# Two-layer group-norm network on one core: both norms two steps later in their bands, the first layer's maps of an image's first band two steps later

## The chip, the cores and the metric

The kernel runs on one core of one Trainium2 chip, in one launch. The metric is the device time of that launch in microseconds (us). Five engines work side by side, each through its own queue in order: PE (TensorE, matrix products), DVE (VectorE), ACT (ScalarE), POOL (GpSimd) and SP (SyncE), which here only issues DMA transfers. [...]

## The reference

The input `x` has 8 images of 256 channels of 64x64 pixels in 32-bit floats. Two layers follow one another, each with a residual:

```python
x = x + _L0_conv_ref(_gn(x), ...)
x = x + _L1_conv_ref(_gn(x), ...)
```

`_gn` is a group norm over 32 groups of 8 channels: every image needs its mean and variance before its first pixel can be normalised.

Layer 0 computes, for every pixel, its own 3x3 filter for each of 32 groups. Two 1x1 maps of 32 channels, `x1` and the 3x3 unfolded `x2`, go through a norm with constants, a relu, a 1x1 convolution to 32 channels ("hidden"), again norm and relu, and a last 1x1 convolution gives 9 weights for each group. The third map `x3` has 256 channels, and the output is the sum of its nine neighbours, each times its weight:

```python
out = jnp.einsum('bgskhw,bgkhw->bgshw', x3u, w)
```

Layer 1 has two branches that are added with rates. One is an attention of 4 heads of 64 channels in which each pixel looks at its 7x7 neighbours (reflected at the rim), with a position term on the keys. The other is a softmax over 9 weights for each channel and pixel, from one 1x1 convolution, that weighs depthwise convolutions (3x3, relu, 3x3) of the layer's input.

## The kernel before, in words

**Tiling.** An image is cut into `NB` = 8 bands of 8 rows, 512 pixels each; 256 channels are two halves of 128 partitions. The main loop runs over `g` = 8 x image + band. While layer 1 works on band `g`, layer 0 is `AHEAD` = 12 bands ahead: in band 0 of an image it makes the maps of band 4 of the next one. The 12 bands before the first (`g` below 0, "alone") have layer 0 only. Both halves and four pieces make 8 steps in a band (`s` = 0 to 7).

**The order is written out by hand.** Nothing is moved by a scheduler: every engine receives its instructions in the order in which the program calls for them. Each step has six places, each ended by `advance()`. `after(n, f)` calls `f` at the n-th place from now. `steer(g, s)` runs at the beginning of a step and starts the norms and the loads of the input. `beside(g, s)` returns two lists of side work for the step: `mid`, called at the third place, whose matmuls are issued there and whose follow-up on ACT or DVE comes a place later; and `end`, called at the last. One entry is an exception: `small_maps` is called where it is appended to `mid`, ahead of the step's score matmuls, and only its follow-up `write_maps` comes with the rest.

**A step in the second layer.** PE multiplies queries with keys (L703) and, for an earlier step, probabilities with values (L747). DVE takes the maximum (L712), ACT the exponential (L720), DVE the reciprocal of the sum (L727), ACT scales the probabilities (L729), and a step later PE transposes them (L735), which ACT copies out (L737). Twice in a step PE makes branch weights `pf` (8 matmul records of 512 columns in all in the trace, L825), and ACT takes their exponential `ex` (L830), which POOL adds up (L1026, L838) and DVE divides (L850). The depthwise convolutions (L773 to L818) are spread over DVE with their first tap and relu on ACT. Side work of layer 1 is the values (L563, with copies of their windows to `vc` on ACT: L572, L577, L581; transposed at L607 and copied at L609), the queries (L637, L641) and the keys (L658; DVE L666 and L673; reflection L683).

**Layer 0 in a band.** `small_maps` multiplies the band with the scaled weights `w12s` (L328), ACT writes the result as eight pieces (L343 or L347), POOL copies their edges (L351 to L358). `value_maps` does the same for each half of `x3` with `w3s` (L369, ACT L374) and stores it to DRAM (L375). `hidden_maps` is called for the band before, with its hidden activations on ACT (L418), the convolution on PE (L429) and what follows at set places later. `values_by_group` loads `x3` back in another layout (L389 to L397, six transfers). `tap_weights` works two bands behind the maps: weights on PE (L447), products on DVE (L460), sums on POOL (L468).

**The norms.** Both use `gn_affine`: DVE joins the statistics (L231), PE averages over groups (L237), DVE works out the variance (L246 to L250), PE again, DVE (L258), ACT takes a square root (L262), DVE the reciprocal and offset (L266, L269). Each stage waits a number of places, the square root standing about 14 places behind the start. `scaled_weights` folds layer 0's norm into its weights: at the end of the chain DVE scales `w12` and `w3` (L296, L297, twice each), PE makes the bias terms (L304), DVE writes them (L312, L314). It is started in band 3, for the image after next. `norm_rows` makes the norm of layer 1 for the next image in band 6; its last steps bring it to every channel (L512 to L524), and the first rows that need it are normalised in bands 7 and 0.

**Buffers.** Nearly all matmul results go through five PSUM buffers with the tag `gen`, used in turn in program order: the next user waits until the reader of the user five places before is done. The scores and the accumulators have PSUM of their own.

The starts of the pieces that the change touches stand in these lines:

```python
if s == (2 if g >= 0 else 3) and i == NB - 2 and 0 <= b + 1 < B:
    norm_rows(b + 1)
n = g + AHEAD + 1
if s == 2 and n % NB == 0 and 0 < n < B * NB:
    scaled_weights(n // NB)
...
if s == 0 and g + AHEAD < B * NB:
    mid.append(small_maps(*divmod(g + AHEAD, NB)))
```

Of the kernel before, what the change touches and what calls it, by code (L numbers as in the profile page):

```python
# [25 lines left out]
NB = H // R  # L26
# [34 lines left out]
AHEAD = NB + 4  # L61
# [25 lines left out]
def conv_layers_kernel(ctx: ExitStack, tc: tile.TileContext, ins: dict, out: bass.AP):  # L87
    nc = tc.nc
    x_in = ins["x"]
    B = x_in.shape[0]  # L90
# [124 lines left out]
    def after(n, f):  # L215
        later.append((place[0] + n, f))
# [399 lines left out]
    def position(b, i):  # L616

        first, last = new_keys(i)
        n, a = last - first, i * R + first
        pe = images[b].pe[i] = w1.tile([P, KW - PAD, W], F32, tag="pe", name=f"pe_{b}_{i}", bufs=1)  # L620
        nc.gpsimd.tensor_add(
            pe[:, :n],
            pecol.unsqueeze(1).to_broadcast([P, n, W]),
            perow[:, a : a + n].unsqueeze(2).to_broadcast([P, n, W]),
        )
# [240 lines left out]
        after(5, quotient)  # L866


    def beside(g, s):

        b, i = divmod(g, NB)
        bn, inx = divmod(g + 1, NB)
        mid, end = [], []

        early = i in (0, NB - 1)
        if g >= 0:
            if s == 2 - early:
                mid.append(lambda: queries(b, i, 1))
            if s == 3 - early:
                mid.append(lambda: keys(b, i, 1))  # L880
        early = inx in (0, NB - 1)
        if 0 <= g + 1 < B * NB:
            if s == 5 - early:
                mid.append(lambda: position(bn, inx))
            if s == 6 - early:
                mid.append(lambda: queries(bn, inx, 0))
            if s == 7 - early:
                mid.append(lambda: keys(bn, inx, 0))

        if g >= 0 and i < NB - 1:  # L890
            if s in (4, 5):
                mid.append(lambda: values(b, i + 2, s - 4))
            if s in (6, 7):
                end.append(lambda: value_tile(b, i + 2, s - 6))
        if g > 0 and i and s in (0, 1):
            mid.append(lambda: value_tile(b, i + 1, s + 2))
        if i == NB - 1 and 0 <= b + 1 < B:
            if s in (4, 5):
                mid.append(lambda: values(b + 1, 0, s - 4))
            if s in (6, 7):  # L900
                end.append(lambda: value_tile(b + 1, 0, 2 * s - 12))
                end.append(lambda: value_tile(b + 1, 0, 2 * s - 11))
        if g >= 0 and i == 0:
            if s == 0:
                mid += [lambda: values(b, 1, 0), lambda: values(b, 1, 1)]
                end.append(lambda: value_tile(b, 1, 0))
            if s in (1, 2):
                mid.append(lambda: value_tile(b, 1, 2 * s - 1))
            if s == 1:
                end.append(lambda: value_tile(b, 1, 2))  # L910

        nxt = [(b, i + 2, 0)] if g >= 0 and i + 2 < NB else []
        if i == NB - 1 and 0 <= b + 1 < B:
            nxt = [(b + 1, 0, 0), (b + 1, 1, 1)]
        for bb, ii, d in nxt:
            if s == d:
                end.append(lambda bb=bb, ii=ii: load_rows(bb, ii))
            if s in (d + 1, d + 2):
                end.append(lambda bb=bb, ii=ii, d=d: normalise(bb, ii, s - d - 1))

        alone = g < 0
        if 0 <= g + AHEAD < B * NB:
            bq_, iq = divmod(g + AHEAD, NB)
            if alone and s == 0:
                mid.append(lambda: small_maps(bq_, iq)())
            if s == (2 if alone else 0):
                (mid if alone else end).append(lambda: value_maps(bq_, iq, 0))
            if s == (3 if alone else 1):
                mid.append(lambda: value_maps(bq_, iq, 1))
        if 0 <= g + AHEAD - 1 < B * NB and s == (2 if alone else 1):  # L930
            at = (3, 7, 8, 12, 16) if alone else (5, 13, 14, 19, 21)
            end.append(lambda: hidden_maps(*divmod(g + AHEAD - 1, NB), at))
        if 0 <= g + AHEAD - 2 < B * NB and s in TAPS_AT[alone]:
            u = TAPS_AT[alone].index(s)
            end.append(
                lambda: tap_weights(*divmod(g + AHEAD - 2, NB), u, g < -1, PRODUCTS_AT[g < -1][u])
            )
        return mid, end

    def steer(g, s):  # L940

        b, i = divmod(g, NB)
        if s == (2 if g >= 0 else 3) and i == NB - 2 and 0 <= b + 1 < B:
            norm_rows(b + 1)
        n = g + AHEAD + 1
        if s == 2 and n % NB == 0 and 0 < n < B * NB:
            scaled_weights(n // NB)
        if s == (3 if g < -1 else 7) and g + AHEAD0 < B * NB:
            first_stats(*divmod(g + AHEAD0, NB), n=40 if g < -1 else 9)
        if s == 5 and 0 <= g + 1 < B * NB:  # L950
            bn, inx = divmod(g + 1, NB)
            xr = images[bn].xr[inx] = x_tile("xr", bn, inx)
            nc.sync.dma_start(out=xr, in_=images[bn].x1[inx].rearrange("(t p) n -> p t n", p=P))
        if s == (0 if g < 0 else 4) and 0 <= g + 1 + AHEAD < B * NB:
            bn, inx = divmod(g + 1 + AHEAD, NB)
            if inx not in images[bn].xc:
                images[bn].xc[inx] = load_x(bn, inx, "xc")
        if s == 5 and 0 <= g - 1 + AHEAD < B * NB:
            values_by_group(*divmod(g - 1 + AHEAD, NB))
        if s == 4 and 0 <= g - 1 + AHEAD < B * NB:  # L960
            x_by_group(*divmod(g - 1 + AHEAD, NB), g < -2)

    with tc.manual_schedule():
# [21 lines left out]
        for g in range(-AHEAD, B * NB):  # L985
            b, i = divmod(g, NB)
            for s in range(STEPS):
                ct, m = divmod(s, NT // 2)
                mid, end = beside(g, s)
                steer(g, s)  # L990
                if g >= 0:
                    if s == 0 and g + AHEAD < B * NB:
                        mid.append(small_maps(*divmod(g + AHEAD, NB)))
                    nm = f"{b}_{i}_{ct}_{m}"
                    sco = score_tile(nm)
                    weighted = [(a, weighted_values(*a, pt, sco)) for a, pt in pending]
                    prob, nmax = scores(b, i, ct, m, sco)
                    for a, po in weighted:
                        add_values(*a, po)
                    pending = [] if before is None else [(before[:-1], transposed(nm, before[-1]))]  # L1000
                    tot = exponentials(nm, prob, nmax)
                advance()
                if g >= 0:
                    ex, exb = w1.tile([P, 2, BAND], F32, tag="ex", name=f"ex_{nm}", bufs=3), ex if m else None
                    branch_weights(b, i, ct, m, 0, ex)
                    if m in (0, 2):
                        todo = list(conv[0])
                    for _ in range(2):
                        todo.pop(0)()
                advance()  # L1010
                if g >= 0:
                    probabilities(prob, tot)
                rest = [f() for f in mid]
                advance()
                for f in rest:
                    if f:
                        f()
                if g >= 0:
                    for _ in range(2 if m % 2 == 0 else len(todo)):
                        todo.pop(0)()  # L1020
                    before = (b, i, ct, m, prob)
                advance()
                if g >= 0:
                    branch_weights(b, i, ct, m, 1, ex)
                    if exb is not None:
                        after(4, lambda ex=ex, exb=exb: nc.gpsimd.tensor_add(ex, ex, exb))  # L1026
                    if m == 1:
                        conv[1]()
                        conv = depthwise_middle(b, i, ct)
                    if m == NT // 2 - 1:  # L1030
                        oc = depthwise_end(b, i, ct, conv[1])
                        after(4, lambda a=(b, i, ct, ex, oc): dynamic_sum(*a))
                if s % 4 == 3 and 0 <= (g * NCT + ct + 1) < B * NB * NCT:
                    gn, cn = divmod(g * NCT + ct + 1, NCT)
                    conv = depthwise_begin(*divmod(gn, NB), cn)
                advance()
                for f in end:
                    f()
                advance()
# [90 lines left out]
```

## Time and profile before

| | |
|---|---|
| median of 3 runs | 4153.6 us (4153.14 to 4155.73) |
| the profiled execution | 4152.64 us |
| its span in the profile | 4150.9 us |
| mean granted clock of PE in it | 0.993 |
| busy PE / DVE / ACT / POOL | 97% / 87% / 74% / 70% |
| a band of image 2, from first score matmul to the next band's | 59.3 to 68.8 us |

The profile is of one execution. Its span runs from the first instruction to the last; the execution's own time has 1.74 us around it. "Busy" is the time in which an engine had an instruction in work, as a share of the span, register and DMA-issuing instructions left out. A line such as L825 is a line of the kernel's file. A group of instructions is named by line, engine, operation and by what it writes and reads; the number of instructions stands behind an x. In the list of waits an engine's idle time is summed by the instruction that ended it: which instruction was late, how often, and the longest of these waits. A line of the timeline gives the start and the duration, the engine and the instruction, and in square brackets the wait ahead of it with what ended it.

### The profile page before, as it was taken

To read this page: it belongs to the slowest core of one execution; us is meant where nothing else is said; L and a number is where in the kernel's file an instruction comes from. 1 tells how busy PE (TensorE), PEld (TensorE's weight loads), DVE (VectorE), ACT (ScalarE), POOL (GpSimd) and SP (SyncE) were. 2 spreads that over 40 slices of the span, in tenths; PEclk is the share of its full clock that TensorE was granted. 3 is DMA by queue.
4 is the path that set the end of the run, shared out by engine and by line. 5 is a ranking of instruction groups with operands and counts; after the bars stand their busy time and mean duration, and the time that the engine had idled before them with its cause. 6 is when DMAs were issued, how large, how long until landed. Compare 5 with 4: busy or idle time off the path is not lost.

```text
span 4150.9 us, 72735 instructions
## 1 busy us (share of the span) xinstructions
PE 4022.6 (97%) x25292; PEld 2126.8 (51%) x25292; DVE 3591.9 (87%) x7248; ACT 3081.0 (74%) x7726; POOL 2923.0 (70%) x1902
## 2 busy tenths in 40 slices
PE   6789999999999999999999999999999999999998
PEld 3345555555555555555555555555555555455554
DVE  5878998899898898889998898888988889977777
ACT  3467778777787777877778777777778777687776
POOL 4767777677786777777777777777777677744554
PEclk8999999999999999999999999999999999999999
DMA  8854234234244233334234234244233233111100
GB/s 226 194 135 111 73 91 109 72 94 109 62 101 107 76 94 98 81 94 109 72 85 118 72 94 105 66 101 106 71 82 99 65 87 85 33 41 39 39 28 21
DMA packets 381264, 367.89 MB, mean 89 GB/s; under 512 B 55648, under 2 KB 282720, under 8 KB 380640
## 3 DMA queue, kind: packets, MB, share of 16 engines
q1 hardware_dynamic: 377568, 358.68, 34.3%
q8 instruction: 200, 3.28, 0.3%
q10 hardware_dynamic: 3328, 4.55, 0.3%
q14 instruction: 168, 1.38, 0.1%
HBM read 261.42 MB, written 101.71 MB: 87 GB/s over the span
## 4 chain that ended last, share of the span: by engine, by line
PE 71%; DVE 14%; POOL 6%; ACT 5%; DMA 2%; issue 2%; SPq 1%; POOLq 0%; ACTq 0%; DVEq 0%
PE pf L825 33%; PE ptp L735 5%; PE sco L747 5%; PE pk L658 5%; PE sco L703 5%; PE p L369 5%; DVE prod L460 4%; PE pq L637 4%; POOL xg L468 3%; PE pvt L607 2%; PE pv L563 2%; DVE acc L808 2%; PE pw L447 2%; DVE acc L782 2%; POOL ex L1026 2%
## 5 line engine op out<-in xcount | busy, mean ns | idle before, releaser
L825 PE MATMUL pf<-yp,c_wfc 128*128 128x512 f32 x4096 | 1930.5, 595 | 10.6 <-ACT vc L581 5.0
L468 POOL TENSOR_TENSOR xg<-xg,prod 128x1024 f32<-128x1024 f32 x549 | 1203.9, 2193 | 96.6 <-DVE prod L460 64.1
L825 PEld LDWEIGHTS pf<-yp,c_wfc 128*128 128x128 f32 x4096 | 729.9, 190 | 690.5 <-issue 619.4
L1026 POOL TENSOR_TENSOR ex<-ex,ex 128x1024 f32<-128x1024 f32 x384 | 907.7, 2364 | 61.9 <-ACT ex L830 57.2
L830 ACT ACTIVATE ex<-pf 128x512 f32<-128x512 f32 x1024 | 607.3, 593 | 297.9 <-POOL ex L1026 141.3
L782 DVE SCALAR_TENSOR_TENSOR acc<-yp,c_chan,acc 128x504 f32<-128x504 f32 (+3 forms) x1104 | 766.2, 694 | 42.3 <-ACT acc L773 21.7
L460 DVE SCALAR_TENSOR_TENSOR prod<-pw,c_par,x3q 128x1040 f32<-128x1040 f32 x576 | 733.9, 1281 | 66.8 <-PE pw L447 21.6
L808 DVE SCALAR_TENSOR_TENSOR acc<-hid,c_chan,acc 128x504 f32<-128x504 f32 (+3 forms) x1024 | 757.8, 740 | 20.2 <-ACT acc L802 2.1
L855 POOL TENSOR_TENSOR ex<-ex,rec 128x512 f32<-128x512 f32 x127 | 162.3, 1278 | 809.5 <-DVE rec L850 767.1
L729 ACT ACTIVATE prob<-prob,tot 128x196 f32<-128x196 f32 x1024 | 411.6, 450 | 387.2 <-DVE tot L727 386.4
L712 DVE CUSTOM_DVE_ANT_0 prob<-sco,c_mask 128x196 f32<-128x196 f32 x1024 | 325.5, 355 | 272.4 <-PE sco L703 272.0
L720 ACT ACTIVATE prob<-prob,nmax 128x196 f32<-128x196 f32 x1024 | 461.4, 454 | 46.9 <-DVE nmax L712 45.3
L747 PEld LDWEIGHTS sco<-pt,vt 112*64 112x64 f32 x8160 | 283.8, 137 | 182.3 <-issue 51.7
L737 ACT COPY pt<-ptp 112x512 f32<-112x512 f32 x511 | 297.0, 581 | 105.0 <-PE ptp L735 103.0
L735 PE MATMUL ptp<-ident,prob 128*112 128x128 f32 x2044 | 341.7, 287 | 31.2 <-ACT prob L729 30.5
L747 PE MATMUL sco<-pt,vt 112*64 112x64 f32 x8160 | 347.0, 227 | 0.0
L735 PEld LDWEIGHTS ptp<-ident,prob 128*112 128x112 f32 x2044 | 203.9, 133 | 201.4 <-issue 77.7
L703 PE MATMUL sco<-kb,qb 64*64 64x196 f32 x4096 | 295.2, 357 | 0.0
L563 PE MATMUL pv<-yp,c_wv 128*128 128x512 f32 (+2 forms) x576 | 247.3, 554 | 0.6
L369 PE MATMUL p<-xc,w3s 128*128 128x512 f32 x512 | 244.4, 601 | 0.0
L658 PE MATMUL pk<-yp,c_wk 128*128 128x512 f32 (+2 forms) x576 | 240.8, 545 | 0.0
L637 PE MATMUL pq<-yp,c_wq 128*128 128x512 f32 x512 | 240.6, 592 | 0.0
(140 smaller groups left out, 5294.0 us busy)
## 6 DMA issues: line engine op xcount, KB each, us to landing
x<-x3n SPq DMA_DIRECT2D x128, 264.0 KB, 2.1
x3q<-x SPq DMA_DIRECT2D x128, 264.0 KB, 7.2
xc<-in_x SPq DMA_DIRECT2D x64, 512.0 KB, 5.0
xg<-in_x SPq DMA_DIRECT2D x256, 128.0 KB, 4.8
x<-xg SPq DMA_DIRECT2D x256, 128.0 KB, 2.4
yp<-x SPq DMA_DIRECT2D x128, 256.0 KB, 3.3
xr<-x SPq DMA_DIRECT2D x64, 512.0 KB, 5.8
out_x<-xr SPq DMA_DIRECT2D x64, 512.0 KB, 3.1
```

What stands on the lines that cost most here:

```text
L369: nc.tensor.matmul(p3, im.w3s[:, kt, mt * P : (mt + 1) * P], im.xc[i][:, kt, :], start=(kt == 0), stop=(kt == NCT - 1),)
L460: nc.vector.scalar_tensor_tensor(prod[:, :, :RUN], pw[:, j, :RUN].unsqueeze(1).to_broadcast([P, SHARE, RUN]), par[:, PCB2 + k : PCB2 + k + 1],
L468: nc.gpsimd.tensor_add(im.xg[i], im.xg[i], rows(prod))
L703: nc.tensor.matmul(sco[half[t], h, :NKEY], qb[half[h], 2 * m + t].rearrange("p r c -> p (r c)"), kb[half[h], :, c0 : c0 + KW], start=True, ...
L720: nc.scalar.activation(prob[:, h, :NKEY], prob[:, h, :NKEY], AF.Exp, bias=nmax[:, h : h + 1], scale=-1.0, accum_out=tot[:, h : h + 1],)
L735: nc.tensor.transpose(ptp[:, h, ch], prob[:, h, ch * CHUNK : (ch + 1) * CHUNK], ident)
L747: nc.tensor.matmul(po[half[h], :, t * TQ : (t + 1) * TQ], im.vt[i + ch, m][:n, t, (2 * ct + h) * HD : (2 * ct + h + 1) * HD], pt[:n, h, ch ...
L782: nc.vector.scalar_tensor_tensor(o, yp[:, ct, ra + dr : rb + dr, ca + dc : cb + dc], chan[:, ct, CW1 + k : CW1 + k + 1], o, ALU.mult, ALU.add,
L808: nc.vector.scalar_tensor_tensor(o, hid[:, ra + dr : rb + dr, ca + dc : cb + dc], chan[:, ct, CW2 + k : CW2 + k + 1], o, ALU.mult, ALU.add,)
L825: nc.tensor.matmul(pf, wfc[:, kt, 2 * m + j, ct * P : (ct + 1) * P], images[b].yp[i][:, kt, PAD : PAD + R], start=(kt == 0), stop=(kt == N ...
L830: nc.scalar.activation(ex[:, j].rearrange("p (r c) -> p r c", r=R), pf, AF.Exp)
L1026: after(4, lambda ex=ex, exb=exb: nc.gpsimd.tensor_add(ex, ex, exb))
```

## The change

Three pieces of work are issued at other steps; no instruction is added, removed or altered.

- `norm_rows` is started at step 4 of band 6 for step 2 (seven bands: images 0 to 6).
- `scaled_weights` is started at step 4 of band 3 for step 2 (six bands: images 0 to 5). In the bands ahead of the first image both stay where they were.
- In band 0 of an image (seven bands, images 0 to 6) `small_maps` goes from step 0 to step 2, the two halves of `value_maps` from the end of step 0 and the middle of step 1 to the middles of steps 3 and 4, `hidden_maps` from the end of step 1 to that of step 3, and `values_by_group` from step 5 to step 6. The other bands keep theirs: `maps_at` returns 0 for them.

```diff
@@ -865,6 +865,10 @@
 
         after(5, quotient)
 
+
+    def maps_at(g):
+
+        return 0 if g % NB else 2
 
     def beside(g, s):
 
@@ -923,11 +927,15 @@
             bq_, iq = divmod(g + AHEAD, NB)
             if alone and s == 0:
                 mid.append(lambda: small_maps(bq_, iq)())
-            if s == (2 if alone else 0):
-                (mid if alone else end).append(lambda: value_maps(bq_, iq, 0))
-            if s == (3 if alone else 1):
+            if alone:
+                at = 2, 3
+            else:
+                at = maps_at(g) + (1 if i == 0 else 0), maps_at(g) + (2 if i == 0 else 1)
+            if s == at[0]:
+                (mid if alone or i == 0 else end).append(lambda: value_maps(bq_, iq, 0))
+            if s == at[1]:
                 mid.append(lambda: value_maps(bq_, iq, 1))
-        if 0 <= g + AHEAD - 1 < B * NB and s == (2 if alone else 1):
+        if 0 <= g + AHEAD - 1 < B * NB and s == (2 if alone else maps_at(g) + 1):
             at = (3, 7, 8, 12, 16) if alone else (5, 13, 14, 19, 21)
             end.append(lambda: hidden_maps(*divmod(g + AHEAD - 1, NB), at))
         if 0 <= g + AHEAD - 2 < B * NB and s in TAPS_AT[alone]:
@@ -940,10 +948,10 @@
     def steer(g, s):
 
         b, i = divmod(g, NB)
-        if s == (2 if g >= 0 else 3) and i == NB - 2 and 0 <= b + 1 < B:
+        if s == (4 if g >= 0 else 3) and i == NB - 2 and 0 <= b + 1 < B:
             norm_rows(b + 1)
         n = g + AHEAD + 1
-        if s == 2 and n % NB == 0 and 0 < n < B * NB:
+        if s == (4 if g >= 0 else 2) and n % NB == 0 and 0 < n < B * NB:
             scaled_weights(n // NB)
         if s == (3 if g < -1 else 7) and g + AHEAD0 < B * NB:
             first_stats(*divmod(g + AHEAD0, NB), n=40 if g < -1 else 9)
@@ -955,7 +963,7 @@
             bn, inx = divmod(g + 1 + AHEAD, NB)
             if inx not in images[bn].xc:
                 images[bn].xc[inx] = load_x(bn, inx, "xc")
-        if s == 5 and 0 <= g - 1 + AHEAD < B * NB:
+        if s == (6 if g >= 0 and i == 0 else 5) and 0 <= g - 1 + AHEAD < B * NB:
             values_by_group(*divmod(g - 1 + AHEAD, NB))
         if s == 4 and 0 <= g - 1 + AHEAD < B * NB:
             x_by_group(*divmod(g - 1 + AHEAD, NB), g < -2)
@@ -989,7 +997,7 @@
                 mid, end = beside(g, s)
                 steer(g, s)
                 if g >= 0:
-                    if s == 0 and g + AHEAD < B * NB:
+                    if s == maps_at(g) and g + AHEAD < B * NB:
                         mid.append(small_maps(*divmod(g + AHEAD, NB)))
                     nm = f"{b}_{i}_{ct}_{m}"
                     sco = score_tile(nm)
```

## The prediction

> **What bounds the kernel now.** I read the page's busy shares first, then the list of waits, then image 2's bands in the timeline. A step is counted from its first score matmul (L703).
>
> ```profile
> PE 4022.6 (97%) x25292; PEld 2126.8 (51%) x25292; DVE 3591.9 (87%) x7248; ACT 3081.0 (74%) x7726; POOL 2923.0 (70%) x1902
> ACT prob L729 <- DVE tot L727: 386.4, 266, 6.4
> POOL x L351 <- ACT x L343: 166.0, 55, 28.2
> ```
>
> PE is the bound; only what lets it idle, or adds to it, moves the end. ACT and DVE wait long in the list, but PE feels that only where the wait reaches it. Windows over band 0 (first line), 1, 3 and 6 of image 2:
>
> ```profile
> 1246.27:1315.04 68.77, 66.73 (x410) 34.84 (x406) 58.05 (x121) 51.42 (x133) 44.85 (x29) 1.00 0.34 84
> 1315.04:1376.60 61.56, 61.07 (x392) 31.99 (x388) 55.31 (x107) 46.61 (x116) 46.72 (x32) 1.00 0.38 93
> 1438.20:1502.10 63.90, 62.73 (x412) 33.60 (x410) 59.70 (x125) 49.20 (x118) 46.85 (x32) 1.00 0.36 90
> 1625.70:1685.00 59.30, 59.20 (x397) 32.90 (x395) 54.84 (x117) 47.95 (x132) 45.88 (x30) 1.00 0.34 82
> ```
>
> After the time come PE, PEld, DVE, ACT and POOL busy. PE is idle 2.04 us in band 0, 0.49 in band 1, 1.17 in band 3, 0.10 in band 6. The bands are in step to a few hundredths across images, so a band's gain or loss counts about seven times (six for the weights' norm). A restart hides a little more: four 512-column records issue in 1.72 us, and against that pace band 0 loses about 3.3 us: 0.6 in step 0, 0.25 in step 5, 1.65 in step 6, 0.8 in step 7. Its worst place and its step 0 in the timeline:
>
> ```profile
> 1298.65 0.81 ACT L729 ACTIVATE prob<-prob,tot 128x196 f32<-128x196 f32 x2 [4.84 <-DVE tot L727]
> 1299.17 0.78 PE L735 MATMUL ptp<-ident,prob 128*112 128x128 f32 x4 [1.44 <-ACT prob L729]
> ...
> 1254.52 0.34 ACT L581 COPY vc<-pv 128x16 f32<-128x16 f32 x3
> 1254.91 0.54 PE L607 MATMUL pvt<-ident,vc 128*112 128x128 f32 x3 [0.15 <-ACT vc L581]
> ```
>
> PE waits for ACT's probabilities (L729), which wait for DVE's reciprocal (L727): DVE is late. In step 0 PE waits for ACT's window copies (L581).
>
> [...] in the scaling of the weights in band 3 (DVE, then POOL beside it):
>
> ```profile
> 1476.16 0.24 DVE L296 TENSOR_SCALAR w12s<-c_w,sc_a 128x64 f32<-128x64 f32 x1
> 1476.32 1.41 DVE L297 TENSOR_SCALAR w3s<-c_w,sc_a 128x256 f32<-128x256 f32 x1
> 1477.65 2.17 DVE L296 TENSOR_SCALAR w12s<-c_w,sc_a 128x64 f32<-128x64 f32 x1
> 1479.74 1.18 DVE L297 TENSOR_SCALAR w3s<-c_w,sc_a 128x256 f32<-128x256 f32 x1
> ...
> 1476.31 1.27 POOL L838 TENSOR_TENSOR ex<-ex 128x512 f32<-128x512 f32 x1
> 1477.54 2.23 POOL L468 TENSOR_TENSOR xg<-xg,prod 128x1024 f32<-128x1024 f32 x1
> 1479.73 1.04 POOL L621 TENSOR_TENSOR pe<-pecol,perow 128x512 f32<-128x512 f32 x1
> ```
>
> Each DVE instruction ends just after a POOL one: 4.76 us for the four. Before POOL is at work, at 25 us, the same four take 0.93. [...] the trace has 1.28 us before Sqrt (L262) and again before the next Exp (L830), so a norm costs ACT 2.77 us wherever it stands.
>
> **The change, part by part.** Nothing is added or removed; instructions change places on all queues. Durations are those of the profiled execution, 4150.9 us of span and 1.74 around it (4152.64); the median of 4153.6 lies 0.96 higher, and the sum is added to the median.
>
> 1. **Maps in band 0** (seven bands). PE loses L328 (0.92 us) ahead of step 0, L369 (1.72) at the end of step 0 and 1.72 in step 1; L328 comes back before step 2, L369 in steps 3 and 4. The hidden maps' matmuls (0.58 and 0.36) go from the ends of steps 3 and 4 to those of 5 and 6. ACT's eight map activations (L343/L347, 463 ns median, 3.82 us in a row) go from step 0 to step 2, x3n (688 ns) and the hidden activations (0.80) two steps later. I walk the queues, keeping durations:
>  - Step 0: the L607 transposes wait for ACT's copies, which end at 1254.75 with no map ahead of them. They stay where they are, so the 0.92 is lost. The two L369 are a gain: step 2 begins 2.56 us earlier, 1.72+1.72-0.92 and rounding.
>  - Step 2: the maps now hold a PSUM buffer of "gen", so the second pf waits for DVE's L673 on the keys: 0.41 us. On ACT the maps stand behind the vt copy of a transpose that PE finishes at 1270.8, and before pf's Exp, L683, L543, L737 and step 3's L720: 71.5+3.8+0.6+0.5+1.1+0.6+1.0, about 1279.1. L720 ended at 1278.7 before. DVE's L727 waits for it in order, with 2.5 us idle, and runs when it ran before (1279.12), while PE is 1.1 us early in step 4. L818 and L773 then come 0.6 later, and so do DVE's taps (1282.6 for 1281.97).
>  - Steps 4 to 6: PE's extra 1.72+0.58-0.36 is eaten by that. L735 of step 6 comes at about 1299.65 (1299.17 before). The next pf now takes the buffer that ACT's vc copies free 2.15 us after L729 begins, so 1301.25, where it began at 1299.78. In return step 7's 0.8 is gone. The band ends near 1316.05 for 1315.04: **+1.0, times 7 = +7**. Bounds: 0 if the buffer wait does not bite, +2 if DVE falls further back.
>  - POOL: the edge copies (L351 to L358) wait in step 2 instead of step 0; POOL waits 3.3 us for a product at 1284.9 anyway, so they cost nothing; without that cover they would delay L838 by their wait.
>  - SP: the two x3n stores come behind the xc and xg loads, and the six x3q loads one step later. They land in 7.2 us (the page's issue list), the first user is some 25 us on: nothing. If SP blocked on a store, the xr load behind it would still have two steps.
>
> 2. **Weights' norm in band 3** (six bands). Two small group matmuls (0.23 each) go from steps 2 and 3 to 4 and 5, the Sqrt with its loads from 4 to 6, the scaling from the start of step 5 to that of step 7, the bias matmuls (L304, 1.35) from 5 to 7. DVE's 0.5+0.95 in step 4 is covered by waits of 0.87 and 0.41 that band 1 shows there. Step 6 keeps a buffer wait on vc (0.85; 0.89 before), the 0.28 ahead of it goes, and the added PE work hides band 1's wait in step 7. But the scaling now meets POOL's chain L468, L1026, L633, L468, without a hole between: about 5.5 us of blocked DVE (bounds 3.0 and 6). Step 7's L712 stands behind it, then L720, L830. The maps' matmul for the next band (L328) waits for that L830's buffer: L712 at 31.7 from step 4's start, L830 ends at 33.7, PE would come at 31.25. So 2.5 us of stall. From step 2 to the next band 50.25 for 48.64: **+1.6, times 6 = +9.6**; -0.9 a band if the block takes 3 us, +2.5 at the other end.
>
> 3. **Rows' norm in band 6** (seven bands). The ends of steps 4 and 5 become lighter on ACT (0.24 of PE stall goes), step 6 gets the 2.77. Its first load falls into ACT's 0.95 of waiting; L729 comes about 0.85 later and the second load delays the vt and pt copies of step 7: two PE stalls of about 0.3 each, and 0.35 from L519 moved there is neutral. **+0.6, times 7 = +4.2**; bounds -0.3 and +1.2. The rows that need the result come in band 7's step 1, a step and a half later.
>
> Sum 7+9.6+4.2 = +21: 4153.6+21 = 4174.6, say 4174. All bounds together: -7 to +37.
>
> **The rivals.**
> - **Faster: the later maps give DVE its time back.** PE has 3.4 us more to do in steps 3 and 4; if DVE uses them, steps 5 to 7 lose nothing: 2.7 a band, of which 2.3 by its own new waits, times 7 = -16, and 4137. For it: the 1.44 us wait is plainly DVE's lateness. Against: ACT's 3.8 us in front of step 3's exponentials. It decides where L727 of step 3 runs within 3.4 us of its scores (3.34 before; my walk has 5.6).
> - **No change:** band 0 gains about 1 us, band 3 pays it back: 4153, within 6 us. For it: no busy time changes.
> - **Slower still:** the scaling also catches a fourth long POOL instruction, and band 0 loses 2: +35, 4189.
> - That the change does nothing is excluded: the compared instruction orders show every move.
>
> **How the numbers follow.** 0.2% is 8.3 us, about what a measurement here can tell from no change. The main case (+9 to +32) gets 0.64, slower still 0.08, no change 0.12, faster 0.16. So slower 0.72, same 0.12, faster 0.16. The range reaches down to the faster case's middle and up to the last: 4140 to 4190; the main case alone has 4162 to 4186.
>
> **What would show it.** Right: band 0 about 1 us longer, its step 2 with a wait of pf for L673, step 3's L727 over 5 us after its scores, step 6's pf waiting for vc; in band 3 the scaling at 5 to 6 us in step 7 and a stall at L328; in band 6 both table loads in step 6. Wrong: band 0 shorter with step 6's wait at L735 under 0.5 us, or the scaling near 1 us.

## The result and the profile after

The changed kernel takes 4187.2 us (median of 4 runs, 4185.5 to 4193.1); the kernel before takes 4154.1 (median of 4 runs, one more than in the table above). The change costs 33 us; the ratio of the runs is 1.0082, with a 95% interval of 1.0064 to 1.0099. The forecast was 4174 in a range of 4140 to 4190, slower by 0.2% with a chance of 0.72. The profiled execution took 4187.25 us, its span is 4185.5.

The busy shares of the page, changed kernel:

```profile
PE 4030.7 (96%) x25292; PEld 2133.6 (51%) x25292; DVE 3610.8 (86%) x7248; ACT 3080.2 (74%) x7726; POOL 2922.8 (70%) x1902
```

Against the kernel before, PE is 8 us busier for the same 25292 records, and DVE 19 us busier for the same 7248. Nothing was added: some matmuls and some DVE instructions took longer. The rest of the loss is idle PE. Windows over bands of the changed kernel, first band 0 of image 1, then bands 0, 3 and 6 of image 2 (length; busy PE, PEld, DVE, ACT and POOL; granted clock, DMA share, GB/s):

```profile
755.37:825.88 70.51, 67.38 (x418) 35.66 (x414) 58.31 (x121) 52.04 (x135) 46.31 (x30) 1.00 0.33 82
1257.81:1330.25 72.44, 69.08 (x419) 36.23 (x415) 58.41 (x121) 52.12 (x135) 47.97 (x30) 0.98 0.33 82
1453.37:1518.68 65.31, 62.62 (x410) 33.69 (x407) 61.26 (x121) 48.53 (x116) 49.17 (x33) 1.00 0.38 96
1643.08:1702.98 59.90, 59.38 (x398) 32.93 (x394) 54.79 (x117) 48.46 (x132) 46.41 (x32) 1.00 0.34 81
```

A window begins at the first score matmul of a band, called the mark here. The small maps of band 0 stood ahead of that mark before and are behind it now, so band 7 of the image ahead is 0.86 us shorter (59.12 for 59.98) and band 0 longer by as much. Net of this, band 0 of image 1 lost 0.87 us (68.78 before) and band 0 of image 2 lost 2.8. They run the same instructions. Most of the difference goes with the granted clock, 1.00 in one and 0.98 in the other.

**Band 0, step 6.** PE's timeline, changed kernel, image 2:

```profile
1311.97 0.78 PE L735 MATMUL ptp<-ident,prob 128*112 128x128 f32 x4 [1.13 <-ACT prob L729]
1313.64 3.24 PE L825 MATMUL pf<-yp,c_wfc 128*128 128x512 f32 x4 [0.89 <-ACT vc L581]
```

PE waits for the late probabilities and then, 0.8 us of work later, for the vc copies to free a PSUM buffer: both waits of the forecast. But the four records behind them take 3.24 us, where the same line takes 1.88 elsewhere. Windows of 3.41 us around this place show why (two of image 1, then two of image 2; same columns):

```profile
809.05:812.46 3.41, 2.26 (x8) 1.14 (x9) 3.37 (x4) 3.31 (x10) 0.45 (x1) 1.00 1.06 207
812.46:815.88 3.42, 3.42 (x10) 1.51 (x9) 3.38 (x9) 2.87 (x8) 3.26 (x3) 1.00 0.02 7
1310.82:1314.23 3.41, 1.40 (x10) 0.72 (x7) 3.37 (x5) 2.71 (x9) 0.00 (x0) 1.00 1.13 201
1314.23:1317.64 3.41, 3.41 (x6) 1.33 (x5) 3.41 (x8) 3.16 (x9) 2.82 (x3) 0.50 0.16 56
```

In image 2 PE was busy for 1.40 us of the first window, and through the whole second one it had half the clock: 6 records where image 1 has 10. The two waits have about the same sum in both images; in image 1 they fall into two windows, in image 2 into one. The half clock begins at 1314.23, 2020.79, 2321.16, 3328.09 and 3631.88 in this profile, and the distances are 207, 88, 295 and 89 times 3.4133 us. In the profile of before the stretches at half clock begin on one such grid as well, from the first at 42.34 us to the one at 3537.59, to 0.01 us. The points 3.41 us apart from them on are called the grid here. The first window of image 2 was not an idle one: 1.40 us of work and 2.0 us of idle time in it were followed by half clock.

**Band 3, step 7.** DVE, then POOL, then PE, changed kernel, image 2:

```profile
1509.43 0.62 DVE L296 TENSOR_SCALAR w12s<-c_w,sc_a 128x64 f32<-128x64 f32 x1
1509.98 2.48 DVE L297 TENSOR_SCALAR w3s<-c_w,sc_a 128x256 f32<-128x256 f32 x1
1512.37 0.52 DVE L296 TENSOR_SCALAR w12s<-c_w,sc_a 128x64 f32<-128x64 f32 x1
1512.81 2.31 DVE L297 TENSOR_SCALAR w3s<-c_w,sc_a 128x256 f32<-128x256 f32 x1
...
1509.95 2.35 POOL L1034 TENSOR_TENSOR ex<-ex,ex 128x1024 f32<-128x1024 f32 x1
1512.81 2.16 POOL L468 TENSOR_TENSOR xg<-xg,prod 128x1024 f32<-128x1024 f32 x1
...
1516.95 1.08 PE L328 MATMUL p<-xc,w12s 128*64 128x256 f32 x8 [1.85 <-ACT ex L830]
1522.05 0.65 PE L607 MATMUL pvt<-ident,vc 128*112 128x128 f32 x4 [0.49 <-ACT vt L609]
```

The four scalings hold DVE from 1509.43 to 1515.12, 5.69 us, each of the long ones about as long as a POOL instruction beside it (2.48 and 2.31 us beside 2.35 and 2.16) and ended 0.16 and 0.15 us after it. The maximum (L712) runs behind them, at 1515.04, the exponential (L720) has waited 4.84 us for it, pf's L830 comes behind, and PE waits 1.85 us for the buffer of the next maps. It pays 0.18 us more just ahead of the next band's first scores and 0.49 in that band's step 0.

**Band 6.** ACT, then PE, changed kernel, image 2:

```profile
1693.69 1.28 ACT L262 ACT_TABLE_LOAD   x1
1695.90 1.28 ACT L830 ACT_TABLE_LOAD   x1
...
1698.76 0.58 PE L519 MATMUL pgc<-both,c_gc 128*128 128x2 f32 x4 [0.48 <-ACT vt L609]
```

The first table load lies in step 6; the second stands ahead of step 6's last exponential and begins 0.49 us into step 7 (1695.41). The vt copy behind it is 0.48 us late for PE.

Where the 34.6 us between the two profiled executions lie:

| place | us |
|---|---|
| band 0, without half clock: 0.81 (mean of images 1, 3, 5, net of the mark) x 7 | 5.7 |
| band 0 of images 2, 4, 6, with half clock: 2.0 (0.25 of it a longer wait), 1.7, 1.8 more | 5.5 |
| band 3 and step 0 of band 4: 1.43 + 0.80 five times, 3.68 in image 3 (half clock there too, and 0.8 shorter before) | 14.8 |
| band 6: 0.56 x 7 | 3.9 |
| up to the end of image 0's band 0, beyond its 0.81 | 5.1 |

The five rows make 35.0. The last row is left apart. The first band of layer 1 begins 1.9 us later, after bands whose order is the same; over the twelve profiles this start lies anywhere from 246.3 to 250.7 us. The band then loses 3.2 us more. In its step 0 PE waits 4.23 us in all (1.87 before), most of it for the copies of its first values, and half clock follows for two windows. That wait alone settles nothing: the kernel with the rows' norm alone, which leaves band 0 as it was, waits 3.02 us there and takes 71.4 us over the band all the same, for 71.3 before. The whole band says more. It takes 71.3 to 71.4 us in the kernel before, in the two with one norm moved and in the one that tests the clock's grid, and 74.8 to 75.4 in the four that move all maps. So the 3.2 us goes with the move of the maps (0.87 of it is the shift of the mark).

### The profile page after: what moved, and what is told of

Read it like the earlier page. It is cut to its first block, busy times and chain, and to the rows that moved or that the text cites. A ratio compares the mean times of both kernels' runs of the same rounds, so it can differ in the third digit from the quotient of the medians.

```text
span 4185.5 us, 72754 instructions
## 1 busy us (share of the span) xinstructions
PE 4030.7 (96%) x25292; PEld 2133.6 (51%) x25292; DVE 3610.8 (86%) x7248; ACT 3080.2 (74%) x7726; POOL 2922.8 (70%) x1902
## 4 chain that ended last, share of the span: by engine, by line
PE 57%; DVE 19%; POOL 11%; ACT 7%; issue 4%; DMA 1%; SPq 1%; POOLq 0%; ACTq 0%; DVEq 0%
PE pf L825 26%; POOL xg L468 7%; DVE prod L460 4%; PE sco L747 4%; PE ptp L735 4%; PE pk L658 4%; PE sco L703 4%; PE p L369 3%; POOL ex L1034 3%; PE pq L637 3%; DVE acc L808 3%; DVE acc L782 3%; DVE rec L846 2%; PE pvt L607 2%; PE pv L563 2%
## 5 line engine op out<-in xcount | busy, mean ns | idle before, releaser
L830 ACT ACTIVATE ex<-pf 128x512 f32<-128x512 f32 x1024 | 607.1, 593 | 277.2 <-POOL ex L1034 126.3
L712 DVE CUSTOM_DVE_ANT_0 prob<-sco,c_mask 128x196 f32<-128x196 f32 x1024 | 325.5, 355 | 253.3 <-PE sco L703 252.5
L720 ACT ACTIVATE prob<-prob,nmax 128x196 f32<-128x196 f32 x1024 | 461.5, 455 | 52.3 <-DVE nmax L712 52.1
L735 PE MATMUL ptp<-ident,prob 128*112 128x128 f32 x2044 | 341.2, 287 | 24.6 <-ACT prob L729 23.9
L735 PEld LDWEIGHTS ptp<-ident,prob 128*112 128x112 f32 x2044 | 204.8, 133 | 192.5 <-issue 78.2
```

Of the source, the lines that this page charges most:

```text
L720: nc.scalar.activation(prob[:, h, :NKEY], prob[:, h, :NKEY], AF.Exp, bias=nmax[:, h : h + 1], scale=-1.0, accum_out=tot[:, h : h + 1],)
L735: nc.tensor.transpose(ptp[:, h, ch], prob[:, h, ch * CHUNK : (ch + 1) * CHUNK], ident)
L830: nc.scalar.activation(ex[:, j].rearrange("p (r c) -> p r c", r=R), pf, AF.Exp)
```

## The experiments

The kernels of one group ran on one chip, with the kernel before among them; "before" is its median there.

**The three parts alone, and half of one** (before: 4156.6 us).

Maps only. Edit against the changed kernel:

```diff
-        if s == (4 if g >= 0 else 3) and i == NB - 2 and 0 <= b + 1 < B:
+        if s == (2 if g >= 0 else 3) and i == NB - 2 and 0 <= b + 1 < B:
-        if s == (4 if g >= 0 else 2) and n % NB == 0 and 0 < n < B * NB:
+        if s == 2 and n % NB == 0 and 0 < n < B * NB:
```

> Only the maps of band 0 go later; both norms stay at step 2. Theory: the three parts add up. Band 0 of images 1, 3 and 5 in the changed kernel is 0.8 us longer than before (70.5 with band 7's last step 0.86 shorter), so the part itself costs 7 x 0.8 = 5.6 us. On top, PE idles 1.13 + 0.89 us in step 6 of band 0, and [...] the next window has half the clock: up to 1.7 us each, in two to four of the seven images. Together +9 to +13: about 4165 us. Rival, the maps alone pay and only their meeting with the norms costs: 4150 or less.

Measured: 4170.0 us, +13.4, ratio 1.0032 (1.0019 to 1.0044), just above what was expected. Its profile has half clock in step 6 of band 0 in five images (0, 2, 3, 5 and 6; two to four expected), where the changed kernel has it in three (2, 4 and 6). The same instructions are hit in other images.

Weights' norm only. Edit against the kernel before:

```diff
-        if s == 2 and n % NB == 0 and 0 < n < B * NB:
+        if s == (4 if g >= 0 else 2) and n % NB == 0 and 0 < n < B * NB:
```

> Only the weights' norm of band 3 goes from step 2 to step 4. Theory: its four scalings meet POOL's chain in step 7 and hold DVE some 5.5 us; PE waits about 1.9 us for the maps' matmul and 0.5 us in step 0 of band 4. That is 1.43 + 0.80 us in the changed kernel, six times: +13.4, and up to one window of half clock more (+1.5): 4167 to 4169 us. Rival, the stall needs the maps of band 0 to be late as well: under 4160.

Measured: 4175.5 us, +18.9, ratio 1.0042 (1.0030 to 1.0055). The part is the costliest, and above the expectation: in its profile all six bands 3 are followed by half clock, where the whole change had one. Without it step 7 and the next band's step 0 take 11.70 + 8.10 us (changed kernel, image 2), with it 11.70 + 8.84 (here, image 2). Here one image follows the other after 501.65 to 501.78 us, and 147 windows of the grid are 501.76: band 3 meets the grid at nearly the same place in every image. That this is why all six meet half clock is my reading; no run moved the bands alone.

Rows' norm only. Edit against the kernel before:

```diff
-        if s == (2 if g >= 0 else 3) and i == NB - 2 and 0 <= b + 1 < B:
+        if s == (4 if g >= 0 else 3) and i == NB - 2 and 0 <= b + 1 < B:
```

> Only the rows' norm of band 6 goes from step 2 to step 4. Theory: 0.56 us in each of seven bands, from the pause of 0.46 us ahead of L519 in step 7: +4, so 4158 us. Rival, the stall of 0.46 is a change of place only (band 6 lost 0.1 before, and band 0 of the next image takes it back): 4154.

Measured: 4159.2 us, +2.6, ratio 1.0008 (1.0000 to 1.0016). Band 6 takes 59.88 for 59.31 us, and band 0 gives nothing back (68.80): the first theory. The run's interval alone would not settle it; the bands do. The three parts alone make +34.9, the change +33: they hardly meet.

The third map only. Edit against the kernel with the maps only:

```diff
-        if 0 <= g + AHEAD - 1 < B * NB and s == (2 if alone else maps_at(g) + 1):
+        if 0 <= g + AHEAD - 1 < B * NB and s == (2 if alone else 1):
-                    if s == maps_at(g) and g + AHEAD < B * NB:
+                    if s == 0 and g + AHEAD < B * NB:
```

> Of the maps of band 0 only the two halves of the third map (3.4 us of PE) go to steps 3 and 4 and its loads to step 6; the small maps stay ahead of step 0 and the hidden maps at step 1. Theory: what spoils the gain is the burst of eight activations (3.8 us of ACT) in step 2 and the 0.92 us of PE lost ahead of step 0; without them DVE gets its work 3.4 us earlier and the wait at L735 in step 6 (1.45 us before) nearly goes: band 0 gains 1 to 2 us, 4140 to 4147 us. Rival, the turn of the PSUM buffers is what costs (the pf of step 6 behind the vc copies): that remains, 4154 to 4160 us.

Measured: 4143.7 us, -12.9, ratio 0.9968 (0.9956 to 0.9981), as the theory has it. Band 0 of image 2 in windows, and its step 6 on PE:

```profile
1248.33:1315.45 67.12, 66.49 (x410) 34.88 (x406) 58.04 (x121) 51.32 (x133) 44.83 (x29) 1.00 0.34 86
...
1299.58 0.78 PE L735 MATMUL ptp<-ident,prob 128*112 128x128 f32 x4
```

67.12 us for 68.77, seven times: -11.6. L735 has no wait in brackets any more. This is the mechanism of the faster rival, in half of the maps' move: step 3's reciprocal (L727) runs 3.36 us after the step's first score, and the forecast named 3.4 as the point from which it decides. In the changed kernel it runs 5.24 us after it (1286.06 to 1291.30), behind the late exponential of ACT, and in step 0 PE waits 1.00 us at the transposes where it waited 0.15 before:

```profile
1291.30 0.17 DVE L727 RECIPROCAL tot<-tot 128x2 f32<-128x2 f32 x1 [2.24 <-ACT prob L720]
...
1265.98 0.32 PE L607 MATMUL pvt<-ident,vc 128*112 128x128 f32 x1 [0.15 <-ACT vc L581]
1267.30 0.54 PE L607 MATMUL pvt<-ident,vc 128*112 128x128 f32 x3 [1.00 <-ACT vc L581]
```

**The other half, and the scalings on ACT** (before: 4157.3 us).

The small maps and the hidden maps only. Edit against the kernel with the maps only:

```diff
-                at = maps_at(g) + (1 if i == 0 else 0), maps_at(g) + (2 if i == 0 else 1)
+                at = 0, 1
-                (mid if alone or i == 0 else end).append(lambda: value_maps(bq_, iq, 0))
+                (mid if alone else end).append(lambda: value_maps(bq_, iq, 0))
-        if s == (6 if g >= 0 and i == 0 else 5) and 0 <= g - 1 + AHEAD < B * NB:
+        if s == 5 and 0 <= g - 1 + AHEAD < B * NB:
```

> The complement of the run with the third map alone: in band 0 only the small maps go to step 2 and the hidden maps to step 3; the third map and its loads stay in steps 0, 1 and 5. Theory: this is the half that costs. PE loses 0.92 us of cover in step 0, the eight activations stand in front of step 3's exponentials, and PE pays in steps 0 and 6: 1 to 2.5 us in each of seven bands, and up to 1.7 us more where the pauses in step 6 fall into one window of the clock's grid: 4163 to 4180 us. Rival, the cost in the full change comes from both halves meeting (five PSUM buffers taken by small and third maps in turn): then this half alone is neutral, 4152 to 4158 us.

Measured: 4188.8 us, +31.5, ratio 1.0076 (1.0064 to 1.0089), dearer than the theory's upper end. Without the third map's 3.4 us of PE in steps 3 and 4, the wait comes a step earlier and longer (step 5 of image 3, PE's timeline):

```profile
1809.86 1.03 PE L735 MATMUL ptp<-ident,prob 128*112 128x128 f32 x4 [1.58 <-ACT prob L729]
```

and half clock follows in all seven bands. The two halves make +31.5 and -12.9, together +18.6; both at once cost +13.4. So the third map's move hid part of what the other half does. The small and the hidden maps were not moved apart from each other; that the small ones are what costs is argued from ACT's burst, which a later run adds by itself.

The changed kernel with the scalings on ACT:

```diff
-                nc.vector.tensor_scalar(im.w12s[:, kt], w12[:, kt], sc[:, kt : kt + 1], None, ALU.mult)
-                nc.vector.tensor_scalar(im.w3s[:, kt], w3[:, kt], sc[:, kt : kt + 1], None, ALU.mult)
+                nc.scalar.activation(im.w12s[:, kt], w12[:, kt], AF.Copy, scale=sc[:, kt : kt + 1])
+                nc.scalar.activation(im.w3s[:, kt], w3[:, kt], AF.Copy, scale=sc[:, kt : kt + 1])
```

> The changed kernel whole, but the four scalings of the weights are made by ACT instead of DVE, at the same place. Theory: what costs in band 3 is that DVE's scalings wait for POOL's instructions (6.1 us for the four, L712 4.85 us late). ACT needs 1.5 to 2 us for them and waits there anyway, so the 1.43 + 0.80 us of band 3 and step 0 of band 4 go, and with them the windows of half clock that follow that stall: 13 to 18 us less than the changed kernel, 4169 to 4174 us. Rival, the norm's extra PE work and its place in step 7 cost by themselves: 4183 to 4188 us.

Measured: 4169.6 us, 17.6 less than the changed kernel's median (which ran in another group); against the kernel before 1.0031 (1.0020 to 1.0041). Two of the four scalings on ACT, image 2:

```profile
1502.12 0.36 ACT L296 ACTIVATE w12s<-c_w,sc_a 128x64 f32<-128x64 f32 x1
1502.37 0.51 ACT L297 ACTIVATE w3s<-c_w,sc_a 128x256 f32<-128x256 f32 x1
```

All four are done in 1.39 us. Band 3 takes 63.14 us (65.31 in the changed kernel, 63.91 before), and the stall at L328 is gone: it came from the blocked DVE. What the norm's later place costs without the block is seen in the next run.

The kernel before with the third map later and the scalings on ACT (both edits as above, both norms at step 2):

> The kernel before with two edits: the third map of band 0 later (as in the run that does that alone) and the scalings on ACT, both norms at step 2. Theory: the third map gives 12.9 us as measured; the scalings hold DVE 4.8 us in step 5 of band 3, and where they took 3.94 us (image 3) the band was 0.8 us shorter, so 0.8 us or a little more in six bands: 4156.6 - 12.9 - 5 = 4139 us. Rival, ACT is short in that step (PE waits there for its vc copies, 0.89 us) and 1.5 to 2 us more of it cost what DVE gains: 4143 to 4150 us.

Measured: 4136.0 us, -21.3, ratio 0.9947 (0.9934 to 0.9959). Band 3 of image 2:

```profile
1432.00:1494.27 62.27, 62.27 (x412) 33.62 (x410) 57.18 (x121) 50.47 (x122) 47.42 (x32) 1.00 0.38 93
```

PE is busy all through (63.91 us before, 1.17 of it idle). It beats both kernels, by 21 and about 51 us. Band 3 gained 1.64 us, twice what was expected. The run before has the scalings on ACT as well, with the norm at step 4. Its band 3 in image 2, and PE's wait in step 6:

```profile
1445.50:1508.64 63.14, 62.47 (x410) 33.63 (x406) 57.01 (x118) 50.71 (x123) 48.36 (x33) 1.00 0.37 92
...
1492.73 1.98 PE L825 MATMUL pf<-yp,c_wfc 128*128 128x512 f32 x4 [0.67 <-ACT vc L581]
```

Bands 1 and 2 ahead of it take 61.6 us each in both kernels. With the scalings on ACT, then, the norm's later place costs 0.87 us a band by itself. Of the 2.23 us that the change lost there, the rest, 1.36, comes with the scalings on DVE, whose block grew from 4.76 to 5.69 us and stands at another place.

**The clock's grid by itself.** In the kernel before, copies on ACT ahead of the probabilities make PE wait in step 6 to 7 of three bands (`spare` is a tile made for them; the lines named here move down by one). If the half clock goes with idle time in one window, as the 2.0 us at 1310.82 in the changed kernel suggest, it should come in these bands too:

```diff
+                    for _ in range({1: 5, 2: 6, 4: 8}.get(i, 0) if s == 6 else 0):
+                        nc.scalar.copy(spare, w3)
                     probabilities(prob, tot)
```

> The kernel before, with 5, 6 and 8 more copies of 512 columns on ACT ahead of L729 in step 6 of bands 1, 2 and 4, so that PE pauses there in every image. A copy issues in 0.53 us and 1.36 us of ACT's waiting take them up, so PE's wait should be about 1.7, 2.3 and 3.3 us for 0.48 us before: 7 x (7.3 - 1.4) = +41 us. Theory of the clock's grid: [...] the whole next window has half the clock, whatever the band. The waits fall on the grid by chance: few of the seven after band 1, some four after band 2 and six or seven after band 4, each with up to 1.7 us more: some +18 us on top, 4215 us. Rival, the half clock comes with what PE does in band 0 and step 7 of band 3, not with idle time: none here, 4197 us.

Measured: 4232.1 us, +74.8, ratio 1.0179 (1.0160 to 1.0197), above both. The waits are longer than I worked out: idle in step 7 is 2.13, 2.64 and 3.94 us, of which 0.48 was there before. Half clock follows in two of seven images after band 1, in seven of seven after bands 2 and 4. Windows of the grid in image 0, two of band 1 and two of band 2:

```profile
369.06:372.48 3.42, 2.24 (x30) 1.24 (x28) 3.35 (x6) 3.18 (x6) 3.34 (x3) 1.00 0.00 0
372.48:375.89 3.41, 2.46 (x8) 1.24 (x9) 3.31 (x9) 3.41 (x9) 3.33 (x3) 1.00 0.00 0
433.92:437.33 3.41, 0.77 (x14) 0.37 (x10) 3.29 (x6) 3.28 (x7) 3.33 (x2) 1.00 0.00 0
437.33:440.75 3.42, 3.42 (x8) 1.71 (x8) 2.26 (x8) 3.04 (x9) 3.42 (x3) 0.50 0.02 5
```

Band 1's 2.13 us are cut in two by the grid and cost 1.65, just their growth; band 2's lie in one window and cost 3.55 for a growth of 2.16. In images 4 and 5 most of band 1's wait (1.85 and 1.67 us) lay in one window as well, and the band took 64.38 and 64.30 us for 63.24. The rival, that half clock belongs to band 0 and band 3, falls. A half-clock window costs 1.1 to 1.4 us here, and about 1.7 in the changed kernel's band 0.

**Two mechanisms of the prediction** (before: 4155.2 us; lines one down in both).

The changed kernel, its scalings on DVE in another form:

```diff
+                    nc.vector.scalar_tensor_tensor(
+                        ws[:, kt], w[:, kt], sc[:, kt : kt + 1], w[:, kt], ALU.mult, ALU.bypass)
```

> The changed kernel whole, the four scalings of the weights still on DVE at the same place, but as scalar-tensor-tensor instructions with the weights as both tensor inputs, the second unused. Theory A: [...] the four take about 1.2 us here too and the time falls as with ACT, to 4169 to 4174 us. Theory B: [...] the block stays and the time with it, 4183 to 4190 us.

Measured: 4198.0 us, ratio 1.0105 (1.0090 to 1.0120). Its first two scalings in image 2:

```profile
1515.46 0.65 DVE L297 SCALAR_TENSOR_TENSOR w12s<-c_w,sc_a 128x64 f32<-128x64 f32 x1
1516.04 2.58 DVE L297 SCALAR_TENSOR_TENSOR w3s<-c_w,sc_a 128x256 f32<-128x256 f32 x1
```

As long as before (0.62 and 2.48 us in the changed kernel): theory B. Why DVE is held beside POOL neither form shows. The time lies above theory B's range; in this profile half clock follows in ten of the thirteen bands 0 and 3 of images 0 to 6 where the change makes PE wait, in the changed kernel's in four. That this is the whole of the difference is not shown.

The kernel before with a burst on ACT and no map moved:

```diff
+                if g >= 0 and i == 0 and s == 2 and b < B - 1:
+                    for _ in range(7):
+                        nc.scalar.copy(spare, w3)
```

> The kernel before, with 7 copies of 512 columns on ACT (0.53 us each, 3.7 us in a row) in step 2 of band 0 of images 0 to 6, at the place where the changed kernel writes its small maps; all maps stay where they were. Theory: this burst ahead of step 3's exponentials is what makes DVE late, as the prediction has it: PE's wait in step 6 (1.45 us before) grows by 2 to 4 us, or comes in an earlier step, plus windows of half clock: +20 to +40 us, 4177 to 4197. Rival, ACT takes the burst up (it is busy 74% of the time) and the cost of the small maps is PE's lost cover in step 0: 4157 to 4163.

Measured: 4178.1 us, +22.9, ratio 1.0054 (1.0037 to 1.0070), inside the theory's range. Two of PE's new waits, image 2, steps 4 and 5:

```profile
1298.18 1.98 PE L826 MATMUL pf<-yp,c_wfc 128*128 128x512 f32 x4 [0.78 <-ACT pt L738]
1303.60 1.98 PE L826 MATMUL pf<-yp,c_wfc 128*128 128x512 f32 x4 [0.89 <-ACT vc L582]
```

Band 0 grows by 3.4 us (72.2 for 68.8): a burst of the same length as the moved activations, at their new place, costs more than the 0.92 us of lost cover. It is extra ACT work here, not moved work, so the 3.4 is not a share of the change. The waits lie steps apart, and in bands 0 of images 1 to 6 no half clock follows.

## Why the prediction was right, and where it fell short

The direction and the three causes held. The loss of 33 us is 12 more than the forecast sum of 21. Without half clock and the extra loss up to the end of image 0's first band, the three parts make 5.7, 13.4 and 3.9 us, 23 in all, near the forecast in part because the errors of the first and the second go opposite ways. The other 12 us, half clock and image 0, stood nowhere in the sum. The range of the main case alone, 4162 to 4186, ends below the measured 4187; the upper end of 4190 was there for a rival whose cause did not come. That the measured time lies within the whole range is to that extent luck.

1. **Band 0, forecast +1.0 a band.** Measured 0.81 where the clock stays whole. The walk's steps are there: step 2 starts 2.58 us earlier (2.56 forecast), step 0 waits 1.15 us for 0.25 (0.92 lost), step 3's L727 comes 5.24 us after its scores (5.6), step 6's pf waits for vc (0.89), step 7 takes 8.15 us for 8.96 (0.8 gone). The wait of step 2's pf for L673 was 0.20, not 0.41. That ACT's burst is what spoils the lead is shown from three sides: the third map alone gains, the small and hidden maps alone lose, the burst alone loses. How much of the loss is the burst and how much the lost cover of step 0 was not measured apart.
2. **Band 3, forecast +1.6.** The block was 5.69 us for "about 5.5", an estimate from the 4.76 us of before and POOL's order in step 7. PE's stall at L328 was 1.85, not 2.5, but the term missed the 0.18 and 0.49 behind it and came to 2.23: mis-sized by 0.6 a band. With the scalings on ACT, which leaves no block, the late norm makes band 3 0.77 us shorter than before, near the 0.9 that the forecast gave for a short block. The walk also took each band as equal across the images; band 3 of image 3 was 0.8 us shorter before (63.11 for 63.9).
3. **Band 6, forecast +0.6.** Measured 0.56, but as one wait of 0.48 ahead of L519 and not as two of 0.3. The "neutral" L519 is where the late vt copy is felt. That the second table load delays it is read from the order on ACT; no run took the load away.
4. **What the sum left out: the clock.** Each wait was priced at its own length. In the changed kernel's profile three bands 0 pay 5.5 us more where half clock comes; with the weights' norm alone six bands 3 meet it. The profile of before could have warned: its clock was whole after image 0's step 0 in spite of 1.44 us of wait in each band 0, but one window at half clock follows 1.77 us of idle time in one window of the grid (image 6, band 4). I read the mean of 0.993 and asked no further.
5. **The rivals.** "Faster" named the right mechanism with too high a price (1.7 a band for 2.7) and was beaten by the burst, as its own condition says. "Slower still" came closest in time (4189), but not by its cause: the block stayed at 5.69 us, and band 0's 2.8 us in image 2 were 0.8 as elsewhere and, for most of the rest, the clock.

Of the 5.1 us up to the end of image 0's first band, the later start of 1.9 stays open. The other 3.2 goes with the move of the maps; why this first band pays more than the later ones is not shown.

## What to carry to other kernels

A step that moves should be split by the queues that it loads: here the same maps were 3.4 us of PE work that was welcome later and 3.8 us of ACT work that was not, and only the first should have moved. Four scalings on DVE took 5.7 us beside POOL's instructions, and 1.4 on ACT. And a wait of PE was not priced at its length alone: 1.13 and 0.89 us of waiting that left PE 1.40 us of work in one window (changed kernel, image 2, 1310.82) were followed by 3.41 us at half clock, which cost about 1.7 us; in image 1 the same two waits fell into two windows (2.80 and 2.26 us of work), and the clock stayed whole.

## What the runs showed of the hardware

Windows here are the stretches of 3.41 us from one point of the grid to the next. In the two kernels' profiles, from 280 to 4080 us after the start, half clock comes six times, each time for one window; ahead of 280 us it also lasts 6.83 and 10.24 us. What the records have of busy PE in the least busy windows at full clock, and the window that followed:

| profile | followed by half clock | followed by the whole clock |
|---|---|---|
| before (1112 windows) | 1.65 us at 3534.17 | 1.84, 1.96, 1.97 us (3592.20, 3291.83, 298.33) and all busier ones |
| changed (1108 windows) | 1.35, 1.40, 1.51, 1.63, 1.66 us (3628.47, 1310.82, 2017.38, 2317.75, 3324.68) | 1.55, 1.56, 1.64, 1.76, 1.90 us (1010.44, 3024.31, 508.68, 2522.55, 1515.62) and all busier ones |

In the run on the clock's grid windows with 0.12, 0.77, 1.09 and 1.56 us were followed by half clock (2597.97, 433.92, 2468.26 and 2403.41), one with 2.24 us (369.06) was not. With the third map alone one with 2.23 us was (488.99), with the weights' norm alone one with 2.75 us (503.35). Busy time as the records have it therefore does not settle which windows are followed by half clock; what does is not shown.

Both forms of scaling on DVE took about the same time beside POOL (2.48 and 2.58 us for 256 columns; in the kernel before 0.35 us at 25.19, where POOL has no work), while ACT did the same columns in 0.51 us in the same step.
